# Two-layer attention kernel on one NeuronCore: layer 1's score maxima become a stream of their own that begins inside layer 0's last rounds

## Chip, core and metric

The kernel runs on one core of one Trainium2 chip. The metric is the device time of one launch in microseconds (us), the median of several runs. Five engines work side by side, each with its own stream of instructions: TensorE (PE in the profile, with its weight loads listed apart as PEld), VectorE (DVE), ScalarE (ACT), GpSimd (POOL) and SyncE (SP, which here only issues DMA transfers). They wait for each other through semaphores.

## The reference

Input `x` is 4 batches of 2048 rows by 256 columns, float32. Two layers follow each other, each of them a layer norm and a sum of two branches added to `x`:

```python
xn = layernorm(x)
x  = x + gated_recurrence(xn) + chosen_heads(xn)     # layer 0
xn = layernorm(x)
x  = x + causal_attention(xn) + channel_mix(xn)      # layer 1
```

- Layer 0, recurrence: two gates `sigmoid(xn @ W + b)`, then a first-order scan over the rows.
- Layer 0, attention: a router picks 4 of 16 heads for each batch; the queries, keys and values of those heads (64 wide) are scaled by a gate; a full softmax attention over 2048 x 2048 scores; the result times `Wo`.
- Layer 1, attention: 16 heads, 16 wide, causal softmax over 2048 x 2048 scores; the result times `W_o`.
- Layer 1, channel mix: `sigmoid(xr @ W_r.T) * (relu(xk @ W_k.T)**2 @ W_v.T)`, where `xr` and `xk` mix each row with the row before it.

## The kernel before

**Batches and stages.** The four batches run one after the other. Each has three stages: the recurrence with the router (`recurrence`, `choose`), the attention of layer 0 (`attention0`), and layer 1 (`layer1`). Everything is float32. A context called `in_order` pins PE, ACT, DVE and POOL to the order in which the Python code issues instructions; the SP queue's order is left to a scheduler. Streams are Python generators: `steps(stream, n)` issues the next `n` pieces of a stream at that place of the order, and that is how work of one stage is woven into another.

**PSUM.** There are eight banks of 128 x 512. `own_bank()` hands them out in turn, all eight; `bank()` does so too but passes over bank 7. In `attention0` bank 7 is the accumulator of the weighted values (`weigh`), so most of its other work uses `bank()`; the streams that belong to layer 1 call `own_bank()`.

**Layer 0's attention.** It works on pairs of row tiles (128 rows each): 4 heads by 8 pairs, 32 pairs in all, in a software pipeline of 34 rounds (`n` from 0 to 33). Round `n` holds the second half of the transposes of pair `n-1` (`turn`, L517, with copies out of PSUM by `keep`, L523), the projection of pair `n-2` (`project`, L555) and its addition to `x` (`add`, L560), then the scores of pair `n` (L495), their maxima (L499) and exponentials (L509), and between them the weighted sums of pair `n-1` (`weigh`, L542, 64 matmuls). In rounds 32 and 33 there is no new pair: these are the draining rounds. From round 27 on the stream `norming` makes the layer norm for layer 1, one block of 512 rows (`q` = 0 to 3) every two rounds: statistics in `add`'s wake (L254, L255), a square root on ACT with a table load before and after it, the scaled rows on DVE (L269), eight transposes on PE (L275) and two copies by ACT (L276). After round 33 comes a loop of eight passes, called the tail below, that takes one step of `norming` and one of `opening` each.

**What layer 1 needs first.** The generator `opening1` makes it, in 24 steps, each a group of matmuls of about equal length and one or two copies by ACT:

- 8 steps of `heads.project(0)`: queries and keys of heads 0 to 7, two steps per block of 512 rows (L688, ACT L690);
- 8 steps of `values1`: the values (L717, ACT L721);
- 8 steps of `heads.project(1)`: queries and keys of heads 8 to 15.

After both steps of a block, `heads.copy` spreads the 16-row heads over strips of 32 partitions, by eight DMAs of the SP queue (L702). Strips are first filled by POOL (`heads.open`, L696). Before the change three of these steps are taken in round 32, three in round 33, eight in the tail, and ten in `layer1`.

**Layer 1's maxima.** For each group of four heads (`g`), each query block (`q`), each of its four row tiles (`t`) and each key block up to the diagonal (`kc`), an object `Maxima` issues for the four heads one matmul of 32 x 128 by 32 x up to 512 (L761; the four stand in four row strips of the array) and one row maximum by DVE. Key blocks off the diagonal use a plain reduction (L767). The diagonal block uses a reduction with a causal mask (L764), 128, 256, 384 or 512 columns wide for `t` = 0 to 3. Such an object, four matmuls and four maxima, is called a unit below. When all units of a `q` are done, their negated maxima are transposed (L829, L832) and written by four DMAs into a spare row of the query strips (L835), so that the later score matmuls (32 rows deep in any case) subtract them within the product.

**Layer 1's attention.** `attending` walks over key tiles: four score matmuls (L786), four exponentials (L788), four weighing matmuls (L797), an addition by POOL (L804). Before it starts, `layer1` issues 20 units of maxima, `4 * NQ + 4`; after that one unit goes with each key tile, so that the maxima stay 20 units ahead. In the code before, those 20 units stand at one place, and the first eight of them alternate with the last eight steps of `opening`:

```python
        ms = maxima()
        for n in range(4 * NQ + 4):
            m = next(ms)
            for h in range(4):
                m.scores(h)
            steps(opening, 1)
            later.slot()
```

## Time and profile before

| | us |
|---|---|
| median of 3 runs | 4306.98 (4306.27 to 4307.82) |
| the profiled execution, own time | 4301.88 |
| its span, first to last instruction | 4300.2 |
| batch 0: round 32's first projection (L688) to the first unit of maxima (L761) | 519.04 to 557.33 |
| batch 0: first unit to the first score matmul of layer 1 (L786) | 557.33 to 602.65 |
| busy share: PE, PEld, DVE, ACT, POOL | 97%, 55%, 72%, 65%, 24% |

Busy shares are averages over stages that differ. The ends of matmuls are modelled in this profile, so PE counts as busy while a matmul is in flight, whether or not the next one could have started. Start times are measured; where they matter below, starts are compared. The other three batches repeat the stretch of batch 0: their first L688 stands at 1580.8, 2641.8 and 3703.8 us and their first L786 at 1664.5, 2725.4 and 3787.6 us.

### The profile page before, as it was taken

What the parts mean: (1) busy time and instruction counts of PE and PEld (TensorE: products, weight loads), DVE (VectorE), ACT (ScalarE), POOL (GpSimd) and SP (SyncE); (2) the same over time, 40 slices, a digit from 0 to 9 for tenths busy, and PEclk for the clock granted to TensorE, in tenths of its full rate; (3) what the DMA queues carried; (4) which work ended last, traced back from release to release, by engine and by line L of the source; (5) the groups of instructions that cost most, each with busy time, mean ns of one, the idle gap of its engine ahead of it and who ended that gap; (6) DMA issues with size and microseconds to landing.
All of it is one profiled execution on the core that took longest, in us unless ns stands there. A gap on an engine that the chain in (4) does not pass through costs nothing.

```text
span 4300.2 us, 86329 instructions
## 1 busy us (share of the span) xinstructions
PE 4189.6 (97%) x32994; PEld 2345.5 (55%) x32994; DVE 3101.0 (72%) x7292; ACT 2809.9 (65%) x6388; POOL 1044.2 (24%) x1322
## 2 busy tenths in 40 slices
PE   6999999999999999999999999999999999999999
PEld 3777653334577764333457776433446766643334
DVE  5767678887577767888657775888856777588882
ACT  3666648886566664888656665588765666568884
POOL 0000015544100001554410000255440000036544
PEclk9999999999999999999999999999999999999999
DMA  3000010100100000010000000001000000100000
GB/s 85 1 11 2 6 17 17 18 25 17 26 1 11 1 9 16 17 37 6 19 24 1 11 1 18 6 17 37 7 19 23 1 11 1 21 5 17 16 7 23
DMA packets 70818, 65.79 MB, mean 15 GB/s; under 512 B 37234, under 2 KB 58628, under 8 KB 68868
## 3 DMA queue, kind: packets, MB, share of 16 engines
q1 hardware_dynamic: 66624, 57.19, 6.1%
q8 instruction: 260, 4.26, 0.4%
q10 hardware_dynamic: 3780, 3.07, 0.2%
q14 instruction: 154, 1.26, 0.1%
HBM read 16.70 MB, written 8.39 MB: 6 GB/s over the span
## 4 chain that ended last, share of the span: by engine, by line
PE 89%; DVE 5%; ACT 3%; issue 1%; POOL 1%; DMA 1%; ACTq 0%; SPq 0%; POOLq 0%; DVEq 0%
PE bank L786 15%; PE bank L761 14%; PE bank L797 12%; PE bank L517 10%; PE bank L495 10%; PE bank L542 10%; PE bank L972 4%; PE bank L291 3%; PE bank L688 3%; PE bank L555 2%; DVE mx L767 1%; PE bank L474 1%; PE bank L457 1%; PE bank L717 1%; PE bank L960 1%; ACT p L509 1%
## 5 line engine op out<-in xcount | busy, mean ns | idle before, releaser
L788 ACT ACTIVATE p<-bank 128x512 f32<-128x512 f32 (+3 forms) x2560 | 1183.1, 539 | 378.9 <-PE bank L786 275.1
L761 PE MATMUL bank<-k,q 32*128 32x512 f32 (+3 forms) x5120 | 1180.9, 584 | 2.2
L767 DVE TENSOR_REDUCE mx<-bank 128x1 f32<-128x512 f32 x1536 | 950.9, 683 | 197.2 <-PE bank L761 196.4
L786 PE MATMUL bank<-q,k 32*128 32x512 f32 (+3 forms) x5120 | 1074.0, 556 | 0.0
L509 ACT ACTIVATE p<-bank,nm 128x512 f32<-128x512 f32 x1024 | 690.4, 686 | 566.5 <-DVE nm L503 566.3
L804 POOL TENSOR_TENSOR o<-o,w 128x512 f32<-128x512 f32 (+3 forms) x576 | 627.0, 1088 | 796.0 <-ACT w L803 795.7
L786 PEld LDWEIGHTS bank<-q,k 32*128 32x128 f32 x5120 | 422.0, 184 | 544.6 <-ACT p L788 409.4
L499 DVE TENSOR_REDUCE mx<-bank 128x1 f32<-128x512 f32 x1024 | 645.9, 683 | 91.4 <-PE bank L495 90.6
L797 PE MATMUL bank<-p,v 128*17 128x512 f32 (+3 forms) x5120 | 601.3, 534 | 21.4 <-ACT p L788 14.3
L764 DVE CUSTOM_DVE_ANT_0 bank<-bank,cmask 128x128 f32<-128x128 f32 (+3 forms) x1024 | 473.1, 523 | 171.3 <-PE bank L761 116.4
L523 DVE COPY pT<-bank 128x512 f32<-128x512 f32 x512 | 353.1, 692 | 286.3 <-PE bank L517 267.9
L761 PEld LDWEIGHTS bank<-k,q 32*128 32x128 f32 x5120 | 473.5, 188 | 139.3 <-DVE mx L767 48.9
L542 PEld LDWEIGHTS bank<-pT,v 128*64 128x64 f32 x8192 | 442.0, 137 | 191.0 <-issue 191.0
L495 PE MATMUL bank<-k,q 64*128 64x512 f32 x2048 | 542.2, 609 | 0.9
L517 PE MATMUL bank<-ident,p 128*128 128x128 f32 x4096 | 490.8, 275 | 20.0 <-ACT p L509 19.8
L542 PE MATMUL bank<-pT,v 128*64 128x128 f32 x8192 | 502.8, 276 | 0.0
L517 PEld LDWEIGHTS bank<-ident,p 128*128 128x128 f32 x4096 | 445.1, 141 | 68.7 <-ACT p L509 29.8
L696 POOL MEMSET q<- 128x2048 f32 x16 | 28.9, 1808 | 1803.8 <-PE bank L542 1803.8
L803 ACT COPY w<-bank 128x512 f32<-128x512 f32 (+3 forms) x576 | 304.9, 529 | 107.2 <-PE bank L797 85.5
L523 ACT COPY pT<-bank 128x512 f32<-128x512 f32 x512 | 293.7, 601 | 55.6 <-PE bank L517 53.9
L797 PEld LDWEIGHTS bank<-p,v 128*17 128x17 f32 x5120 | 88.7, 95 | 439.8 <-ACT p L788 237.1
L495 PEld LDWEIGHTS bank<-k,q 64*128 64x128 f32 x2048 | 212.5, 188 | 170.0 <-issue 83.4
(164 smaller groups left out, 3346.7 us busy)
## 6 DMA issues: line engine op xcount, KB each, us to landing
x<-in_L_attn_x_dram SPq DMA_DIRECT2D x20, 512.0 KB
q<-q SPq DMA_DIRECT2D x64, 128.0 KB
vals<-o SPq DMA_DIRECT2D x256, 32.0 KB
out_dram<-x SPq DMA_DIRECT2D x32, 256.0 KB
q<-qp SPq DMA_DIRECT2D x48, 128.0 KB
k<-kp SPq DMA_DIRECT2D x48, 128.0 KB
q<-nmT SPq DMA_DIRECT2D x256, 2.0 KB
q<-qp SPq DMA_DIRECT2D x64, 32.0 KB
```

The source lines that it names most:

```text
L495: PE.matmul(self.s[j][i], lhsT=self.qT[i][half_, self.t * P:(self.t + 1) * P], rhs=self.kT[half_, j * QB:(j + 1) * QB], start=True, stop=True)
L499: DVE.tensor_reduce(self.mx[:, n:n + 1], self.s[j][i], AX.X, ALU.max)
L509: ACT.activation(self.p[j][:, i, :], self.s[j][i], AF.Exp, bias=nm, accum_out=self.sums[:, n:n + 1])
L517: PE.transpose(self.tr[j][i][:, n * P:(n + 1) * P], self.p[j][:, i, n * P:(n + 1) * P], ident)
L523: copy(self.pT[:, n0:n0 + 4, :], self.tr[j][i].rearrange("p (n q) -> p n q", q=P))
L542: PE.matmul(acc[i * DH:(i + 1) * DH, 0:P], lhsT=self.v[h][:, N * j + n, self.k * DH:(self.k + 1) * DH], rhs=tile_.pT[:, 8 * h + N * j + n, ...
L761: PE.matmul(s[:, 0:n], lhsT=self.qT[strip(h), self.qs], rhs=self.kT[strip(h), self.ks], start=True, stop=True)
L767: DVE.tensor_reduce(self.mx[:, h, :], s[:, 0:n], AX.X, ALU.max)
L786: PE.matmul(s[:, c0:QB], lhsT=self.kT[strip(h), self.ks], rhs=self.qT[strip(h), self.q0 + c0:self.q0 + QB], start=True, stop=True)
L788: ACT.activation(p[:, h % 2, c0:QB], s[:, c0:QB], AF.Exp, scale=SC1)
L797: PE.matmul(acc[32 * h:32 * h + DH1 + 1, c0:QB], lhsT=self.v[h], rhs=self.p[h // 2][:, h % 2, c0:QB], start=True, stop=True)
L804: POOL.tensor_tensor(self.o[:, c0:QB], self.o[:, c0:QB], w[:, c0:QB], ALU.add)
```

## The change

The maxima leave `layer1` and become a class `Leading`, which counts the units it has handed out. `attention0` is given that object and issues units itself: four in round 32 (one after the first steps of `opening`, one after the projections, one before each half of `weigh`), one in round 33, and one in each of the eight passes of the tail, 13 in all. `layer1` then issues units only until the count reaches 20, which are seven, with one step of `opening` beside each.

So that data are there for them, `opening` starts earlier: two of its steps are taken in round 29 and two in round 31 (`NA * NP - 3` and `NA * NP - 1`). Its order changes too: three pieces of `values1` now follow the second block of projections, three the third and two the fourth. In the tail the step of `opening` and the unit come before the step of `norming`; before, `norming` came first.

Finally, `own_bank` and `bank` become one function, which passes over bank 7 while `attention0`'s rounds run and not otherwise. The tail and everything outside `attention0` use all eight banks.

No matmul, reduction, copy or DMA is added or dropped; they change place.

```diff
-    turn = [0]
+    turn, summing = [0], [False]
 
     def own_bank():
         turn[0] = (turn[0] + 1) % 8
+        if summing[0] and turn[0] == 7:
+            turn[0] = 0
         return banks[turn[0]]
 
-    def bank():
-
-        if own_bank() is banks[7]:
-            own_bank()
-        return banks[turn[0]]
+    bank = own_bank
...
+        summing[0] = True
...
             steps(norming, 1)
+
+            if n in (NA * NP - 3, NA * NP - 1) or n >= NA * NP:
+                steps(opening, 2)
             if n >= NA * NP:
-                steps(opening, (2, 2)[n - NA * NP])
+                leading.lead()
...
+            if before and new is None:
+                leading.lead()
             if new:
                 a.scores(0)
...
             if before:
+                if new is None:
+                    leading.lead()
                 before.weigh(0)
...
             if before:
+                if new is None:
+                    leading.lead()
                 before.weigh(1)
...
         steps(background, 100)
+        summing[0] = False
         for _ in range(8):
+            steps(opening, 1)
+            leading.lead()
             steps(norming, 1)
-            steps(opening, 1)
         steps(norming, 100)
...
-        for q in range(NQ):
-            if q == NQ - 1:
-                for _ in range(6):
-                    steps(valuing, 1)
-                    yield
+        for q, count in enumerate((0, 3, 3, 2)):
             for _ in range(2):
                 steps(projecting, 1)
                 yield
             heads.copy(0, slice(q * QB, (q + 1) * QB))
+
+            for _ in range(count):
+                steps(valuing, 1)
+                yield
         for i in range(2):
             heads.open(1, i)
         heads.copy(1, slice(0, T))
-        projecting = heads.project(1)
-        for _ in range(2):
-            steps(valuing, 1)
-            yield
-        yield from projecting
+        yield from heads.project(1)
...
+    class Leading:
+        def __init__(self, b, qk):
+            self.b, self.qk, self.count = b, qk, 0
+            self.units = self.all()
...
+        def next(self):
+            self.count += 1
+            return next(self.units, None)
+
+        def lead(self):
+            m = self.next()
+            for h in range(4):
+                m.scores(h)
...
-        ms = maxima()
-        for n in range(4 * NQ + 4):
-            m = next(ms)
-            for h in range(4):
-                m.scores(h)
+        while leading.count < 4 * NQ + 4:
+            leading.lead()
             steps(opening, 1)
-            later.slot()
...
-            m = next(ms, None)
+            m = leading.next()
```

`Leading.all` and `Leading.turn`, left out here, hold the former `maxima` and `turn_maxima` of `layer1` unchanged.

More of the change, by code (lines that the diff above doesn't have):

```diff
@@ L560, in add, with attention0 @@
                 DVE.scalar_tensor_tensor(xs, ps[:, 0:D], tile_.rc, xs, ALU.mult, ALU.add)
-    def attention0(b, xT, xt, ch, recurring, first, v, rest_of_values, norm, opening):
+    def attention0(b, xT, xt, ch, recurring, first, v, rest_of_values, norm, opening, leading):
         NP = NT // 2
@@ L804, in weigh, with all, turn, layer1 @@
                 POOL.tensor_tensor(self.o[:, c0:QB], self.o[:, c0:QB], w[:, c0:QB], ALU.add)
-    def layer1(b, heads, vs, opening, x1, prepare):
+    class Leading:
+        def __init__(self, b, qk):
+            self.b, self.qk, self.count = b, qk, 0
+            self.units = self.all()
+        def all(self):
+            for g in range(NG):
+                for q in range(NQ):
+                    mx = sm.tile([P, 4, 4, q + 1], FP, tag="mx1", name=f"mx1_{self.b}_{g}_{q}",
+                                 padded_shape=[P, 4, 4, NQ])
+                    for t in range(4):
+                        for kc in range(q + 1):
+                            yield Maxima(q, t, kc, *self.qk[g], mx)
+                    self.turn(g, q, mx)
+        def turn(self, g, q, mx):
+            nm, qT = nms[q % 2], self.qk[g][0]
+            DVE.tensor_reduce(nm[:, 0:16].rearrange("p (h t o) -> p t h o", h=4, o=1), mx, AX.X, ALU.max, negate=True)
+            row = sm.tile([P, 32], FP, tag="nmT", name=f"nmT_{self.b}_{g}_{q}")
+            DVE.transpose(row, nm)
+            for j in range(4):
+                to = qT[DH1:P:32, q * QB:(q + 1) * QB].rearrange("h (t r) -> h t r", t=4)[:, :, 32 * j:32 * j + 32]
+                SP.dma_start(to, row[32 * j:32 * j + 16, :])
+        def next(self):
[5 more added lines that the diff above has]
+                m.scores(h)
+    def layer1(b, heads, vs, opening, x1, prepare, leading):
         xT = heads.xT
@@ L813, in layer1 @@
         mix = ChannelMix(b, xT, x1, vals)
-        def maxima():
-            for g in range(NG):
-                for q in range(NQ):
-                    mx = sm.tile([P, 4, 4, q + 1], FP, tag="mx1", name=f"mx1_{b}_{g}_{q}",
-                                 padded_shape=[P, 4, 4, NQ])
-                    for t in range(4):
-                        for kc in range(q + 1):
-                            yield Maxima(q, t, kc, *qk[g], mx)
-                    turn_maxima(g, q, mx)
-        def turn_maxima(g, q, mx):
-            nm, qT = nms[q % 2], qk[g][0]
-            DVE.tensor_reduce(nm[:, 0:16].rearrange("p (h t o) -> p t h o", h=4, o=1), mx, AX.X, ALU.max, negate=True)
-            row = sm.tile([P, 32], FP, tag="nmT", name=f"nmT_{b}_{g}_{q}")
-            DVE.transpose(row, nm)
-            for j in range(4):
-                to = qT[DH1:P:32, q * QB:(q + 1) * QB].rearrange("h (t r) -> h t r", t=4)[:, :, 32 * j:32 * j + 32]
-                SP.dma_start(to, row[32 * j:32 * j + 16, :])
         def attending():
@@ L1048, in two_layers @@
             heads, vs = Heads1(b, norm.xT), []
+            leading = Leading(b, heads.strips)
             opening = opening1(b, heads, vs)
-            attention0(b, xT, xt, ch, recurring, (q0, k0), v, valuing, norm, opening)
+            attention0(b, xT, xt, ch, recurring, (q0, k0), v, valuing, norm, opening, leading)
             mixing, norming, choosing = layer1(b, heads, vs, opening, x1,
-                                               lambda: prepared(b + 1, ready) if b + 1 < B else NOTHING)
+                                               lambda: prepared(b + 1, ready) if b + 1 < B else NOTHING, leading)
         steps(mixing, 100)
```

## The prediction, written before the changed kernel was run

> **What bounds the kernel now.** I read the page first, for who carries the span; then busy time by stage ("windows"), because the page's shares are means over stages; then the chain of waits over one seam between the layers, for when each group of matmuls starts.

> ```profile
> span 4300.2 us, 86329 instructions
> PE 4189.6 (97%) x32994; PEld 2345.5 (55%) x32994; DVE 3101.0 (72%) x7292; ACT 2809.9 (65%) x6388; POOL 1044.2 (24%) x1322
> ...
> PE 89%; DVE 5%; ACT 3%; issue 1%; POOL 1%; DMA 1%; ACTq 0%; SPq 0%; POOLq 0%; DVEq 0%
> ```

> TensorE carries the chain nearly everywhere, so a reordering gains only where TensorE really waits. The 97% can't say where that is: ends of matmuls are modelled. The windows can (us; PE, PEld, DVE, ACT, POOL busy with counts; clock; DMA):

> ```profile
> 519.04:557.33 38.29, 37.17 (x198) 25.02 (x197) 7.16 (x23) 16.54 (x36) 3.55 (x2) 1.00 0.11 26
> 557.33:578.87 21.54, 21.54 (x98) 7.92 (x97) 15.51 (x58) 5.46 (x9) 0.00 (x0) 1.00 0.37 54
> 578.87:602.65 23.78, 23.66 (x96) 17.15 (x97) 22.56 (x60) 1.97 (x2) 0.00 (x0) 0.68 0.01 1
> 3763.70:3787.60 23.90, 23.78 (x97) 17.26 (x97) 22.72 (x60) 1.97 (x2) 0.00 (x0) 0.68 0.01 1
> ```

> Row 1 is rounds 32, 33 and the tail: VectorE works 7.16 of 38.29 us. Row 2 is the eight units of maxima that alternate with projections. Row 3 is the other twelve units, alone: VectorE works 22.56 of 23.78 us and sets the pace. The last row is the same stretch of the last batch; the two between agree to 0.1 us. What TensorE needs for those twelve is read from starts in the chain of waits (start, us, what):

> ```profile
> 538.41 1.30 PE bank L275 x4
> ...
> 541.88 8.63 PE bank L717 x40
> ...
> 557.40 0.43 PE bank L761 x8
> 557.83 1.91 PE bank L688 x4
> 559.74 0.65 PE bank L761 x8
> 560.39 1.91 PE bank L688 x4
> 562.30 0.86 PE bank L761 x8
> 563.16 1.91 PE bank L688 x4
> 565.07 1.07 PE bank L761 x8
> 566.14 1.91 PE bank L688 x4
> ...
> 580.77 22.07 PE bank L761 x67
> ```

> A unit takes TensorE 0.43, 0.65, 0.86 or 1.07 us by its width (128 to 512), and a projection beside it 1.91. On VectorE the timeline has four plain 512-wide maxima in 2.48 us; masked ones start 0.25, 0.38, 0.52 and 0.65 us apart. So a unit and a projection together (2.98) are TensorE's pace, and a unit alone (1.07 against 2.48) is VectorE's. The twelve lone units are nine of 1.07, one of 0.86, one of 0.65, one of 0.43: 11.6 us of TensorE in 23.8. **12.2 us a batch are idle, four times a launch.** The other idle of the seam is before the transposes of the last norm block: in the same chain VectorE's `add` (L560) starts at 535.43 and the transposes at 538.41, and these take 1.30 at VectorE's pace against 0.44 for the next four: some 1.8 us.

> **The change part by part.**

> *Moved, none added:* instruction counts on every engine stay. Thirteen units go from `layer1` into rounds 32, 33 and the tail; four opening steps go into rounds 29 and 31.

> *Rounds 29 and 31.* Two projections take 3.54 to 3.63 us (chain: 3.63 at 531.12). Those rounds start with back-to-back transposes (32 in 3.64 us at 473.41), so there is nothing to fill: +3.6 each, with 0.1 for the broken run, +7.3. The wait for ACT's table loads in these rounds (1.4 us before 489.05 and 1.2 before 517.71) comes after the inserted work and stays. ACT's two copies (0.69 each) stand before the round's exponentials, while TensorE has over 5 us of transposes and scores: nothing. The 16 SP transfers and two POOL memsets (1.80 each) go with them; POOL is idle there (4.17 of 45.63 us), and SP's next user is the strips, wanted one or two rounds later (a strip copy of eight issues takes 4.9 us). The strips come from the pool of 14 buffers that also holds the transposed weights; in the changed order each first write to such a buffer still comes after the `weigh` that freed it, already issued on TensorE ahead of the transposes that are copied, so I cost the pool at nothing. With one buffer fewer that cover would be gone, at 1.9 us (32 matmuls of `weigh`) a round.

> *From round 32's first opening step to layer 1's first score matmul, TensorE only*, with 1.73 a values step (8.63 for five), 0.1 at each change of kind:
> - Round 32: two values 3.55, unit 0.53, transposes 1.75, norm 0.53, `project` 0.63, unit 0.74, values 1.83, unit 0.96, half of `weigh` 1.9, unit 1.17, half 1.9: 15.5.
> - Round 33: two projections 3.54, unit 1.17, `project` 0.63, values 1.83: 7.2.
> - Tail: values 1.72, unit 0.53, norm 0.53, values 1.83, unit 1.17, norm 0.44, then projection or values with a unit (1.91 each; units 0.65, 1.07, 0.86, 1.07, 1.07, 1.07): 6.2 + 11.5 + 5.8 = 23.5.
> - `layer1`: two projections and a unit 4.7, then with three units 1.91 x 4 + 0.43 + 1.07 + 1.07 = 10.2, then three lone units 0.65 + 1.07 + 1.07 = 2.8: 17.7.

> Sum 63.9. The stretch is 83.6 now (519.04 to 602.65).

> *What VectorE adds.* Its new work is in FIFO with the drain of layer 0. In round 32 its second unit waits behind `add` and the statistics (2.1 us), so the third unit's last bank is late by 0.4. In round 33 a 2.48 us unit stands before `add`. From that unit's scores: 0.5 to the first result, 2.48, 3.0 from `add` to the norm transposes (535.4 to 538.4), and 1.30 for these at VectorE's pace: 7.3. TensorE has until then the unit, `project`, two values steps, the next unit and the transposes themselves, 6.4. They end 0.9 late, where it is 1.8 now. From the second unit to the last VectorE has 45 us of work in 57. Then the first score matmul meets VectorE as it does now, with two units queued. So 63.9 + 0.4 + 0.9 = 65.2.

> *Banks.* Seven instead of eight for the units of two rounds: followed bank by bank, the waits are those just counted. The turned maxima (four DMAs) now precede the third block's strip copies on SP by about 2.6 us; those are wanted 20 us later.

> A batch saves 83.6 - 65.2 - 7.3 = **11.1 us**; four give **44 us**. From the other side: 12.2 + 1.8 idle now, less 1.3 of new waits and nine more alternations at 0.19 (1.91 against 1.72), is 11.0.

> [...] The row first: while units run alone, PEld is busy 17.15 of 23.78 us, 72%, and while they alternate 7.92 of 21.54, 37%. [...] But the groups of the two windows (alternating, then lone) have the same loads at 182 and at 254 ns:

> ```profile
> L761 PEld LDWEIGHTS bank<-k,q 32*128 32x128 f32 x65 | 2.7, 182 | 6.4 <-DVE mx L764 3.8 <-DVE mx L767 1.5 <-issue 1.1
> ...
> L761 PEld LDWEIGHTS bank<-k,q 32*128 32x128 f32 x96 | 17.1, 254 | 7.3 <-DVE mx L767 3.6 <-DVE mx L764 1.9 <-issue 0.2
> ```

> The share is swollen by slow loads, not by more work, so I take the starts.

> The row for the clock: 0.68 in the lone stretch, 1.00 in the alternating one. [...]

> **The rivals.** The point from which a difference is told from none is 0.2%, 8.6 us.

> 1. *As worked out*: -44 us, **4263**. Between 9 and 13 us a batch (all idle of now is 14.0): 4255 to 4271.
> 2. *VectorE hands the wait back.* Its queue holds units before `add`, the statistics and the copies of transposes; if each of the five units of rounds 32 and 33 makes TensorE wait 1 to 1.5 us for a bank, 5 to 7 us a batch go: -16 to -24, 4283 to 4291. For: 7 banks, and a masked 512 unit holds them 2.6 us. Against: only 7.16 us of VectorE work in 38 now.
> [...]
> [...]

> **How the numbers follow.** Rival 1: 0.78; 2: 0.11, faster too; 4: 0.04, half of it within 0.2%, a quarter either side; 3: 0.07. Faster by over 0.2% 0.90, within 0.02, slower 0.08. The range takes rival 1 with its bounds and the near half of rival 2: 4250 to 4284. The profiled execution's own time is 4301.88, 1.7 over its span and 5.1 below the median of the runs; the 44 us are a difference, applied to the median of 4306.98: 4263.

> **What would show it.** The stretch from round 32's opening to the first L786 should be 65 us and not 83.6, with only three lone units and no 24 us at a clock of 0.68; VectorE busy about 25 of the first 40 us; rounds 29 and 31 longer by 3.6 us each; the attention of layer 1 as long as now. The prediction is wrong if L761 shows waits for maxima in rounds 32 and 33, if the norm transposes come more than 2 us late, or if the clock drops in the tail.

## The result and the profile after

The changed kernel takes 4265.66 us (median of 4 runs, 4263.87 to 4266.27), the kernel before 4306.62 us (4305.65 to 4307.82): a ratio of 0.9905, 95% interval 0.9892 to 0.9917. That is 41.0 us less; 44 were forecast. The profiled execution of the changed kernel took 4265.95 us with a span of 4264.2. Against the profiled execution of before (span 4300.2) that is only 36.0 us, because the latter lay 4.7 us below the median of its runs.

The page's shares hardly move, which is why they could not have shown the gain:

```profile
PE 4155.7 (97%) x32994; PEld 2300.1 (54%) x32994; DVE 3103.7 (73%) x7292; ACT 2809.0 (66%) x6388; POOL 1044.7 (25%) x1322
...
PE 89%; DVE 5%; ACT 3%; issue 1%; POOL 1%; DMA 1%; ACTq 0%; SPq 0%; POOLq 0%; DVEq 0%
```

The windows of batch 0 (us; PE, PEld, DVE, ACT, POOL busy with counts; clock; DMA) show it. The first row runs from the transposes that open round 29 to round 32's first opening step, the second from there to the first score matmul of layer 1 (now L792):

```profile
474.94:527.44 52.50, 49.90 (x393) 33.11 (x393) 34.97 (x84) 34.12 (x80) 0.65 (x3) 1.00 0.05 11
527.44:592.95 65.51, 64.81 (x373) 34.85 (x374) 45.81 (x141) 21.05 (x43) 3.55 (x2) 1.00 0.15 25
```

The first row's stretch was 45.63 us before, the second's 83.61. So 6.87 us went in and 18.10 came out: 11.2 us for this batch, and the clock is 1.00 throughout. The 38.29 us of drain in which VectorE was busy for 7.16, and the 23.78 us at a clock of 0.68, have become one mixed stretch.

The chain of waits over that stretch (start, us, what) has the new order, unit (L767) beside step (L698 projections, L727 values; L540 is `weigh`):

```profile
534.41 0.80 PE bank L767 x8
535.21 1.92 PE bank L727 x8
537.14 0.98 PE bank L767 x8
538.12 1.90 PE bank L540 x32
540.02 1.07 PE bank L767 x8
...
547.73 2.47 DVE mx L773 x4
550.19 0.78 DVE x L558 x2
...
553.10 1.30 PE bank L273 x4
554.40 1.73 PE bank L727 x8
...
586.91 1.07 PE bank L767 x8
587.99 1.91 PE bank L698 x4
589.90 3.09 PE bank L767 x23
```

The pace is the 2.98 us (1.07 and 1.91) of the old alternation. The one place where the chain leaves TensorE is round 33: a unit's four maxima (2.47 us) stand before `add` (now L558) on VectorE, and the norm transposes (now L273) start 2.91 us after `add`. The last line is the three units that still stand alone.

By stage, from the starts of matmuls in the traces (means of the four batches, us; the kernels below are those of the experiments):

| kernel | first score matmul of layer 0 to first of layer 1 | from there to the last unit |
|---|---|---|
| before | 502.7 | 400.7 |
| changed | 491.7 | 402.2 |
| e1_early_only | 504.5 | 401.7 |
| e2_tail_only | 496.1 | 401.2 |
| e3_spread | 490.5 | 399.2 |
| e4_no_early | 492.3 | 402.5 |
| e5_late_spread | 490.3 | 399.3 |

In the first column the change earns 11.0 us a batch. In the second, which the prediction took as unchanged, it loses 1.5. In all four batches that is 43.9 less 6.1, or 37.8 us. Outside the two columns 1.8 are lost: 0.9 ahead of batch 0's first score, 0.5 between the batches, 0.4 at the end. That leaves the 36.0 us between the profiled executions. The start of batch 0's first score lies anywhere from 99.4 to 101.6 us in the seven traces, so its 0.9 is within the scatter of that start. Where the other 4.7 us of a typical execution of before lie, no trace shows.

### The profile page after: what moved, and what is told of

Its sections match the earlier page's. It is cut to its first block, busy times and chain, and to the rows that moved or that the text cites. A ratio compares the mean times of both kernels' runs of the same rounds, so it can differ in the third digit from the quotient of the medians.

```text
span 4264.2 us, 86371 instructions
## 1 busy us (share of the span) xinstructions
PE 4155.7 (97%) x32994; PEld 2300.1 (54%) x32994; DVE 3103.7 (73%) x7292; ACT 2809.0 (66%) x6388; POOL 1044.7 (25%) x1322
## 4 chain that ended last, share of the span: by engine, by line
PE 89%; DVE 5%; ACT 3%; issue 1%; POOL 1%; DMA 1%; ACTq 0%; SPq 0%; POOLq 0%; DVEq 0%
PE bank L792 15%; PE bank L767 13%; PE bank L803 12%; PE bank L515 10%; PE bank L493 10%; PE bank L540 10%; PE bank L989 4%; PE bank L698 3%; PE bank L289 3%; PE bank L553 2%; DVE mx L773 1%; PE bank L472 1%; PE bank L455 1%; PE bank L977 1%; DVE mx L497 1%
## 5 line engine op out<-in xcount | busy, mean ns | idle before, releaser
L767 PE MATMUL bank<-k,q 32*128 32x512 f32 (+3 forms) x5120 | 1138.7, 569 | 1.7
L792 PE MATMUL bank<-q,k 32*128 32x512 f32 (+3 forms) x5120 | 1075.4, 557 | 0.0
L792 PEld LDWEIGHTS bank<-q,k 32*128 32x128 f32 x5120 | 422.9, 184 | 547.1 <-ACT p L794 407.0
L540 PEld LDWEIGHTS bank<-pT,v 128*64 128x64 f32 x8192 | 441.9, 137 | 193.2 <-issue 193.2
L540 PE MATMUL bank<-pT,v 128*64 128x128 f32 x8192 | 503.7, 276 | 0.0
L767 PEld LDWEIGHTS bank<-k,q 32*128 32x128 f32 x5120 | 430.8, 184 | 129.5 <-DVE mx L773 42.4
```

Of the source, the lines that this page charges most:

```text
L540: PE.matmul(acc[i * DH:(i + 1) * DH, 0:P], lhsT=self.v[h][:, N * j + n, self.k * DH:(self.k + 1) * DH], rhs=tile_.pT[:, 8 * h + N * j + n, ...
L767: PE.matmul(s[:, 0:n], lhsT=self.qT[strip(h), self.qs], rhs=self.kT[strip(h), self.ks], start=True, stop=True)
L792: PE.matmul(s[:, c0:QB], lhsT=self.kT[strip(h), self.ks], rhs=self.qT[strip(h), self.q0 + c0:self.q0 + QB], start=True, stop=True)
```

## Experiments

The theory: TensorE stood idle where units of maxima stood alone, at VectorE's pace; the gain is that idle time, filled by setting units beside other matmuls. The main rivals: the gain comes from starting projections early; VectorE takes back in rounds 32 and 33 what is filled; and, for the 1.5 us lost in layer 1, that a lower granted clock of TensorE takes it.

**Early projections alone (e1_early_only).** Every `leading.lead()` in `attention0` and its tail is taken out; the early steps stay.

```diff
-            if n >= NA * NP:
-                leading.lead()
...
-            if before and new is None:
-                leading.lead()
...
-                if new is None:
-                    leading.lead()
...
             steps(opening, 1)
-            leading.lead()
             steps(norming, 1)
```

> The changed kernel with the early projections kept, but no unit of maxima before layer1: all 20 stand there again, beside 4 steps of opening instead of 8. Theory (the gain is TensorE idle time filled by units; starting projections early earns nothing): rounds 29 and 31 stay 3.4 us longer each, and now 16 units stand alone at VectorE's pace instead of 12. Idle grows by about 8 us a batch against the kernel before, less 4 alternations of 0.19: about 7 us a batch slower than before, 4335 us (4320 to 4345). Rival (the early projections carry the gain, since they thin out the drain): below 4290 us. Rival (both parts are needed and neither alone does anything): 4300 to 4312.

Measured: 4312.97 us (4310.13 to 4316.05), ratio to before 1.0014 (1.0008 to 1.0021). It is slower than before, so the early start alone earns nothing and costs; but it is 6.3 us slower and not 28. This kernel also keeps the new order of `opening`, the new order of the tail and the one rule for the banks, so none of these carries the gain: only the places of the units differ, and they are worth 47.3 us. The stages say why it is not slower still. Rounds up to the last score of layer 0 are 6.9 us longer, as expected. From there to layer 1's first score it takes 85.1 us, where before took 90.2, although 16 units and not 12 stand alone. The window from the first unit to that score, and three pieces of the chain of waits over it (VectorE's masked maxima, the transposed maxima, then units to the end):

```profile
562.40:604.30 41.90, 41.42 (x176) 27.21 (x177) 37.82 (x118) 4.72 (x6) 0.00 (x0) 0.76 0.07 8
```

```profile
571.27 0.68 DVE bank L761
...
574.21 0.21 DVE nmT L826
...
575.04 29.39 PE bank L758 x92
```

The 20 units now take 41.90 us with four projections among them; before they took 45.32 with eight. TensorE needs 17.8 for the units and 1.91 for each projection, so it idles 16.5 here and 12.2 before: 4.3 more, not 8. I had set VectorE's 35.3 us for 16 units against TensorE as if the last of them had to be finished before layer 1 begins. The trace has 73 of their 80 maxima done when the first score matmul goes out, and the last ends 4.0 us later (batch 0; in the kernel before 73 and 4.1). The sign was right, the size was off by a factor of four, and by the numbers I had written down the run lies just beyond the band of the rival that says neither part does anything alone. The run does count against the rival that the early start carries the gain.

**Units in the tail alone (e2_tail_only).** As e1, with `leading.lead()` kept in the tail: eight units there, 12 in `layer1`, eight of these alone.

> The changed kernel with units in the eight passes of the tail alone, none in rounds 32 and 33; 12 are left for layer1, eight of them alone. Theory: idle is what the lone units leave: eight units take VectorE about 14 us after the two queued ones, TensorE 7.5, so 6.5 us a batch come back, less 1 for five fewer alternations and 0.9 for the waits of rounds 32 and 33: about 4.6 us a batch slower than the changed kernel, 4284 us (4277 to 4291). Rival (units in front of layer 0's additions and statistics cost about what they fill): 4258 to 4270.

Measured: 4280.75 us (4277.17 to 4281.52), ratio to before 0.9941 (0.9924 to 0.9958). From layer 0's first score to layer 1's it takes 4.3 us a batch more than the changed kernel (496.06 against 491.74); 4.6 were expected. Lone units cost what was worked out for them, and the five units of rounds 32 and 33 earn far more than the waits they cause. In the chain the same alternation stands, and at its end the lone units with VectorE as releaser:

```profile
576.01 1.92 PE bank L690 x4
577.92 1.11 PE bank L759 x8
579.03 0.68 DVE bank L762
...
582.18 2.97 DVE mx L765 x5
...
585.20 9.79 PE bank L759 x32
```

**No early projections (e4_no_early).** As e2, and the two steps of rounds 29 and 31 are taken out as well; `layer1` has eight steps of `opening` for its 12 units, so four stand alone.

```diff
-            if n in (NA * NP - 3, NA * NP - 1) or n >= NA * NP:
+            if n >= NA * NP:
                 steps(opening, 2)
```

> The changed kernel without the four early projection steps in rounds 29 and 31, and with units in the eight passes of the tail alone; layer1 has 12 units and 8 steps of opening, so 4 units stand alone. Theory (moving projections earlier is neutral, TensorE was full in those rounds; what counts is how many units stand alone): rounds 29 and 31 give back 6.9 us a batch, the drain takes them again, and one more lone unit than in the changed kernel costs at most 1.7: 4264 to 4272 us. Rival (the early start is what makes the gain): as slow as with 12 lone units, 4290 us or more.

Measured: 4267.59 us (4265.57 to 4268.26), ratio to before 0.9908 (0.9892 to 0.9925), within 2 us of the changed kernel. The early steps of the change are neutral: what they take out of the drain they put into two full rounds. The two differ by one lone unit and by the five units of rounds 32 and 33, and their first column by 0.6 us.

**No unit alone (e3_spread).** The changed kernel with one more unit in round 33, and the last six units each behind one of the last six steps of `opening`.

```diff
             if n >= NA * NP:
                 steps(opening, 1)
+                if not before:
+                    leading.lead()
...
         xT = heads.xT
-        steps(opening, 2)
...
         while leading.count < 4 * NQ + 4:
-            leading.lead()
             steps(opening, 1)
+            leading.lead()
```

> The changed kernel with no unit alone: one more unit in round 33, and the last six beside the last six steps of opening (step first, then unit). Theory (the first score matmuls of layer 1 meet a VectorE with two units queued, TensorE then idles, and its clock drops to half for one or two windows of 3.4 us, which costs layer 1 up to 2.4 us a batch): the clock stays at 1.00 there, the time from the first L792 to the last L767 goes back from 401 to 403 us to about 400, and three more alternations cost 0.6: 1.5 to 3 us a batch less, 4254 to 4260 us. Rival (the longer layer 1 has another cause, such as the shifted banks): 4265 to 4268.

Measured: 4247.69 us (4247.57 to 4248.73), ratio to before 0.9864 (0.9848 to 0.9881): 18 us below the changed kernel, more than the 6 to 12 expected. The first column falls by 1.2 us a batch where I expected a cost of 0.6: lone units still left TensorE waiting. The second falls by 3.0. These are the windows of layer 1's first 10 us in the changed kernel (batch 0, then parts of batches 1 and 3):

```profile
592.95:596.30 3.35, 3.35 (x13) 1.60 (x12) 3.35 (x7) 1.19 (x2) 0.41 (x1) 1.00 0.00 0
596.30:603.10 6.80, 6.80 (x31) 3.88 (x28) 5.47 (x14) 3.15 (x6) 1.22 (x3) 0.50 0.00 0
...
1651.00:1654.40 3.40, 3.40 (x19) 3.20 (x18) 2.53 (x10) 1.49 (x4) 0.41 (x1) 0.51 0.00 0
...
3751.10:3758.10 7.00, 7.00 (x35) 3.90 (x32) 7.00 (x17) 3.82 (x7) 1.22 (x3) 1.00 0.00 0
```

the same stretch in this experiment (batch 0):

```profile
590.60:594.00 3.40, 3.40 (x23) 1.66 (x18) 3.18 (x7) 3.30 (x5) 0.42 (x2) 1.00 0.00 0
594.00:600.80 6.80, 6.80 (x56) 3.15 (x55) 5.88 (x14) 4.46 (x11) 2.06 (x6) 1.00 0.01 2
```

and in the kernel before (batch 0):

```profile
602.65:606.00 3.35, 3.35 (x17) 2.42 (x12) 3.35 (x6) 1.09 (x2) 0.09 (x1) 0.71 0.00 0
606.00:612.80 6.80, 6.80 (x51) 3.40 (x51) 5.88 (x16) 4.60 (x10) 1.81 (x5) 1.00 0.00 0
```

The count in brackets is of matmuls in flight. In the changed kernel 13 are in the first 3.35 us (10 of them start there) while VectorE is full with the queued units; then the clock is 0.50 for 6.8 us with 31 matmuls. In e3 it is 23 (19 start), a clock of 1.00, and 56. In the kernel before the clock comes into layer 1 at half, as it left the stretch of lone units (0.68 over that stretch), and goes up to 1.00 (0.71 over the first 3.35 us, then 1.00). The batches differ in how long the clock was down behind layer 1's first score. Where it fell only behind that score, or not at all, the second column goes with it (us, from the traces):

| batch | clock at 0.5 | first score of layer 1 to last unit |
|---|---|---|
| e2, 3 | 0 | 400.7 |
| changed, 3 | 0 | 400.8 |
| e4, 0 | 3.4 | 401.5 |
| changed, 1 | 3.4 | 402.0 |
| changed, 2; e1, 2 and 3 | 6.8 | 402.8 |
| e4, 1 | 6.8 | 402.9 |
| e4, 3 | 6.8 | 403.2 |
| changed, 0 | 6.8 | 403.3 |
| e3 and e5, all eight | 0 | 399.1 to 399.4 |

Each 3.4 us at half clock go with about 1 us more, not the 1.7 that half of it would be. The batches of one kernel issue the same units and scores in the same order, and where their clock did not differ behind the score (e3, e5) they lie within 0.3 us of each other, so here the clock is the likely cause of the differences; no run changed it alone. Batches in which the clock was already down at that score lie off this line: before (1.6 to 2.3 us: 400.5 to 400.9), e1's first two (0.7 and 1.4: 400.7 and 400.6), e2's first three (9.5, 6.9, 2.9: 402.6, 401.2, 400.4) and e4's batch 2 (9.5: 402.4). Without any half clock behind the score (batch 3) the changed kernel still needs 1.6 us more than e3. Its last queued maximum ends 4.1 us after the first score, that of e3 2.7 us after it, and the difference fits that remainder; it was not measured apart.

**No unit alone and no early projections (e5_late_spread).** From e3: the early steps and the four units of round 32 taken out; two units in round 33, eight in the tail, ten in `layer1`, each beside a step.

```diff
-            if n in (NA * NP - 3, NA * NP - 1) or n >= NA * NP:
+            if n >= NA * NP:
                 steps(opening, 2)
-            if n >= NA * NP:
+            if n > NA * NP:
                 leading.lead()
```

> Without the early projections in rounds 29 and 31, with two units in round 33, eight in the tail and ten in layer1, each beside a step of opening (step first): no unit stands alone. Theory (all that counts is that every unit has other TensorE work beside it; where the projections start is neutral): the same as with the early projections and no lone unit, first score of layer 0 to first L78x/79x of layer 1 490 to 491 us, no clock below 1.00 at the start of layer 1, 399 us from there to the last unit: 4244 to 4251 us. Rival (the early start and the units in round 32 are worth something of their own): 4255 us or more.

Measured: 4246.97 us (4246.08 to 4247.37), ratio to before 0.9863 (0.9847 to 0.988). Nothing in rounds 29, 31 and 32 is needed. The stretch from the first unit to layer 1's first score, and what follows, of batch 0:

```profile
533.70:589.30 55.60, 55.60 (x277) 25.86 (x280) 43.87 (x131) 16.17 (x33) 0.00 (x0) 1.00 0.19 32
589.30:592.70 3.40, 3.40 (x23) 1.66 (x17) 3.17 (x7) 3.31 (x5) 0.42 (x2) 1.00 0.00 0
```

This and e3 beat both kernels. At 4247.7 and 4247.0 us they are not told apart, so the early steps are neutral here too.

## Why the prediction was right, point by point

- **The idle time.** 12.2 us of lone units and 1.8 before the norm transposes were to be had. The two together bound the gain at 14.0 a batch; e3 and e5, in which no unit is alone, take 12.2 and 12.4 in the first column.
- **Rounds 29 and 31**: 7.3 us forecast, 6.87 measured. As said, nothing was there to fill, and e3 and e5 together show that the move is neutral.
- **Round 32 to layer 1's first score**: 65.2 forecast, 65.5 measured, and two small errors in it nearly cancel. Round 32 took 15.6 in the chain (527.41 to 542.99); its sum without waits was 15.5, so hardly any of the forecast 0.4 is there. The norm transposes were forecast to end 0.9 late. In the trace they start 0.7 late, behind the 2.47 us of maxima before `add`, and end about 1.3 late (554.24, where the unit before them, started at 551.90, would have let them end by 552.9). The clock stays at 1.00 in drain and tail (the row of 65.51 us) and the time fell by 41.0 us, so no run gives a ground for the chances numbered 3 and 4 (0.07 and 0.04). VectorE was busy for 26.3 of the first 40 us; about 25 was forecast.
- **The share of weight loads or the starts.** The runs decide for the starts: 12.2 us a batch were read from them as idle, and the first column fell by 11.0, in e3 and e5 by 12.2 and 12.4. PEld was busy 72% of a stretch in which half of TensorE's time was free (17.15 and 12.2 of 23.78 us), and it is 53% in the stretch that replaced it (34.85 of 65.51).
- **The clock** was weighed at the wrong place. I asked whether the tail would lose its clock (it does not: 1.00). "The first score matmul meets VectorE as it does now" came true: in both kernels 73 of the 80 maxima are done at that moment, and in batch 0 the last ends 4.13 us later. The step that failed is what was taken from it, "the attention of layer 1 as long as now", in which the clock had no term. Before, the clock came into layer 1 at half and was at 1.00 within 1.6 to 2.3 us. In the changed kernel it comes in at 1.00 and falls in three of four batches, 3.5 to 4.0 us behind the first score, to 0.50 for 3.4 or 6.8 us. Those batches took 1.5 to 2.4 us more there than the same batches before, the fourth 0.1. The sum, 6.1 us, is the way from the 44 forecast (43.9 in the first column) to the 37.8 of the two columns; the prediction's bounds for its first rival, 9 to 13 a batch, take it in.
- **The strips' buffers, the banks, SP and POOL** were costed at nothing. The chain of waits over the new stretch names no DMA and no POOL there.

## What to carry to other kernels

When one engine is always busy in the records, look for stretches in which starts are further apart than the same instructions' starts elsewhere: that is idle time (here 12.2 us a batch), and it is filled by setting each piece of the slower engine's work beside work of the faster one. Moving work between two stretches in which the busy engine is full gained nothing (e4: 4267.59 us against 4265.66; e5: 4246.97 against 4247.69); what counts is how many pieces stand alone, and also how much the slower engine still has queued when the next stage begins. A few lone pieces at a seam can come with more than their own wait: behind the changed kernel's three the clock was 0.50 for 3.4 or 6.8 us in three of four batches, and in e3 and e5, which have none, in no batch.

## What the runs showed of the hardware

In batch 0 of the changed kernel 10 matmuls, all 32 rows deep, start in the 3.35 us from 592.95, no two neighbours more than 0.54 us apart, at a clock of 1.00; 6.8 us at 0.50 follow. In e3 19 start in 3.40 us, and the clock stays at 1.00 (56 matmuls in flight in the next 6.8 us).
